# Row gathers and key projections moved across a branch in a single-core layer kernel

## The chip, the cores and the metric

The kernel runs on one core of a Trainium2 chip. A core has five engines with an instruction stream each: PE (TensorE, the matrix multiplier), DVE (VectorE), ACT (ScalarE), POOL (GpSimd) and SP (SyncE, which only issues transfers here). They meet through semaphores, and 16 DMA engines move data between the device memory (DRAM) and the core's on-chip memory. The metric is the device time of one execution in microseconds (us), as the median of several runs.

## The reference

The input is x, 4 sequences of 512 rows of 512 numbers (2048 rows), and a context of 4 x 512 rows of 256. Four blocks each add their result to x:

```python
x = x + ssm(ctx, layernorm(x))              # state space scan over the context
x = x + moe(layernorm(x))                   # 64 experts, 8 chosen for each row
x = x + attention(layernorm(x), ctx)        # 16 heads of 128, keys and values from ctx
x = x + ternary_ffn(layernorm(x))           # 512 -> 2048 -> 512, quantized weights
```

The change lies at the seam of the second and the third. In the second, each row has eight choices k = 0 to 7, and its result is a sum over them:

```python
y   = ragged_dot(silu(gate) * up, down)     # rows sorted by expert
out = zeros_like(x).at[tok].add(y * w[:, None])
```

In the third, keys and queries are projected, normalized by the root of their mean square over a head (gains gk and gq), and multiplied:

```python
q, k = rmsnorm(q, gq), rmsnorm(k, gk)
attn = softmax(einsum('bqhd,bkhd->bhqk', q, k) / sqrt(128))
out  = einsum('bhqk,bkhd->bqhd', attn, v) @ Wo
```

## The kernel before, in words

x stays on chip for the whole kernel as `x_all`, 16 tiles of 128 rows. The kernel goes through the state space block, then the routing, then a loop over experts (`Experts.run_in`, i = 0 to 65). In pass i it loads rows and weights of expert i + 2 by gathers on POOL (tiles `xg0`, `xg1`, `wg`, `wd`, four buffers each), multiplies gate and up for expert i - 1 (`gate_up`, L1343) and down for expert i - 2 (`down`, L1367 to L1389). The results are copied from the accumulators to tiles `yo` by DVE and ACT and stored by SP to a DRAM table `y_dram`, sorted by expert. An expert has room for a fixed number of rows.

Rows that did not fit are handled behind a branch: every engine loads the number `many` (L771) and takes the branch `tc.If(many > 0)` (L772) past that block, which is not executed with these inputs. On the way each engine waits for the transfers it depends on, and the first instructions behind the branch that share data wait until the other engines have passed it.

Then comes `attend`. It must first add the experts' results to x: for each tile t and choice k a gather on POOL brings 128 rows of `y_dram` (256 KB) into a tile `yg` (`fetch`, L1883), and DVE multiplies them by the router's weight and adds them to x (`add`, L1891). For the first four tiles these are 32 gathers and 32 additions. With all eight added, `stats` takes a tile's mean and variance on DVE (L1897, L1899) and the inverse deviation on POOL (`ve_c` L1901, `rstd_c` L1903), and `normed` writes `xn_c` on DVE (L1909).

A second kind of work fills PE meanwhile. The keys of sequences 2 and 3 for heads 8 to 15 (`KEYS_LATE`, 16 pairs) are left over from earlier. One key task is: the projection on PE (`pk`, L1223), its square `k_sq` and its scaled copy `k_kT` on ACT (L1232, L1233), a store of `k_kT` to `k_dram` (256 KB, L1234), the sums of squares on PE (`kpss`, L1243), and their copy `k_ms` on ACT (L1255). `k_sq` and `k_kT` are read out of the accumulator after pk, so kpss follows one task behind.

The order of the front of `attend` is written by hand: `later(time, f)` puts a step at a nominal time, the steps are sorted by it and issued in that order, so that each engine executes its part of them in that order, whatever the real times are. The plan has eight key tasks at a pace of 2.6 (`some_keys`), the gathers from 3.0 on at a pace of 1.35 (`GAP`), each addition 6.0 behind its gather (`FLIGHT`), and from 21.0 (`FRONT`) on four windows of 14.5 (`WINDOW`), one per tile of sequence 0. A window i holds `turn_x` (four transposes of xn_c, L1916), a key task, two projections of queries of four heads each (`queries`, L1962, with a 1 MB weight Wq for each), the norm of them (`norm_q`: `qms` on DVE, `rq` on POOL L1974; `scale_q`: `qn` on DVE L1980), their transposes (`turn_q`: `pqt` on PE L1989, copied to `qT` by ACT L1990), a second key task, and scores, softmax weights and their transposes for the first head (`scores` L1996, `weights`, `turn`). SP loads Wq for both groups (`load_q`), and keys, inverse norms and values of a head (`load_kv`: `kT`, `rk`, `v`, 256 KB each). Then the main loop over heads follows, and the ternary block is laid into it.

The first landing places of the gathers are four slices of a tile `yg_first` and eight of two tiles `yg_more`, which have other uses later; the others go through four buffers `yg`. `ms` holds the keys' mean squares of all sixteen late tasks.

Of the kernel before, what the change touches and what calls it, by code (L numbers as in the profile page):

```python
# [17 lines left out]
F32 = mybir.dt.float32  # L18
# [41 lines left out]
HG = 4  # L60

KEYS_LATE = [(b, h) for b in (2, 3) for h in range(8, H)]
DH = 2048
RESET = 1e30
MAGIC = 12582912.0
# [54 lines left out]
class Plan:  # L120
# [618 lines left out]
@with_exitstack  # L739
def moe_phase(ctx, cm, x_all, w, kv, dr, router_stats, out):  # L740

    tc, nc = cm.tc, cm.nc
    order = ctx.enter_context(ExitStack())
    order.enter_context(tc.manual_schedule())
    ssm_phase(cm, x_all, w, kv, router_stats)
    keep = ctx.enter_context(tc.tile_pool(name="b_keep", bufs=1))
    dp = ctx.enter_context(tc.tile_pool(name="b_dram", bufs=1, space=DRAM))
    y_dram = dp.tile([ROWS[E], DM], F32, name="y_dram")
    z_dram = dp.tile([NOV * P, DM], F32, name="z_dram")


    r = dict(wk=keep.tile([P, NT, TOPK], F32, name="wk"),
             pos=keep.tile([P, NT, TOPK], I32, name="pos"),
             nov=keep.tile([E, 1], F32, name="nov"),
             room=keep.tile([E, 1], F32, name="room"),
             many=keep.tile([1, 1], I32, name="many"))
    tern = Ternary(cm, keep, w)


    late = ctx.enter_context(tc.tile_pool(name="b_late", bufs=1))  # L760
    with ExitStack() as es:
        more = es.enter_context(tc.tile_pool(name="b_more", bufs=1))
        r["tok"] = more.tile([P, 3, E], I32, name="tok")
        r["widx"] = more.tile([P, E], I32, name="widx")
        keys = Keys(cm, w, kv, cm.k_small, None, None, None)
        with tc.tile_pool(name="e_w", bufs=4) as wp:
            ex = Experts(cm, w, dr, y_dram, r, wp)
            route(cm, x_all, w, dr, router_stats, r, more, late, keys, ex)
            ctx_k = ex.run(tern, more, late, keys, kv)
        order.close()  # L770
        many = nc.values_load(r["many"][0:1, 0:1], min_val=0, max_val=NOV)  # L771
        with tc.If(many > 0):  # L772
            rest(cm, x_all, w, dr["xn"], z_dram, r, many)
    with tc.manual_schedule():
        attend(cm, x_all, w, kv, y_dram, r["wk"], r["pos"], tern, late, ctx_k, keys.wk, out)


@with_exitstack
# [415 lines left out]
class Keys:  # L1194
# [6 lines left out]
    def __init__(self, cm, w, kv, small, row, psum, ctx, direct=None):  # L1201


        self.cm, self.nc, self.w, self.kv = cm, cm.nc, w, kv
        self.small, self.row, self.psum, self.ctx, self.direct = small, row, psum, ctx, direct
        self.wk = {}
        self.pk = self.sq = self.pss = None

    def load(self, h0, h1, pool, tag, queue=None):
# [17 lines left out]
    def evict(self):  # L1227
        if self.pk is None:
            return
        b, h, pk = self.pk  # L1230
        sq, kT = self.row("sq"), self.row("kT")
        self.nc.scalar.activation(sq, pk, AF.Square)  # L1232
        self.nc.scalar.activation(kT, pk, AF.Copy, scale=self.cm.gkq)  # L1233
        self.nc.sync.dma_start(self.kv["k"][b, h], kT)  # L1234
        self.pk, self.sq = None, (b * H + h, sq)

    def squares(self):
# [154 lines left out]
class Experts:  # L1392
# [20 lines left out]
        if FIRST <= i < E:  # L1413
            f(self.st[i])

    def run(self, tern, more, late, keys, kv):


        with ExitStack() as es:
            return self.run_in(es, tern, more, late, keys, kv)  # L1420

    def run_in(self, ctx, tern, more, late, keys, kv):
        cm, ex, st = self.cm, self.ex, self.st
        tc = cm.tc
        ex.sp = ctx.enter_context(tc.tile_pool(name="e_s", bufs=2))
        ex.yp = ctx.enter_context(tc.tile_pool(name="e_y", bufs=3))
        ex.ps = ctx.enter_context(tc.tile_pool(name="e_ps", bufs=2, space=PSUM))
        ex.pg = ctx.enter_context(tc.tile_pool(name="e_pg", bufs=3, space=PSUM))
        ex.po = ctx.enter_context(tc.tile_pool(name="e_po", bufs=3, space=PSUM))
        ex.tp = ctx.enter_context(tc.tile_pool(name="e_xt", bufs=1))  # L1430
        tp = ctx.enter_context(tc.tile_pool(name="e_t", bufs=2))
        ctx_k = late_contexts(keys, self.w, late)
        slots, norms = slot_tasks(cm, self.dr, kv, self.r, more, ex.ps)
        halves = tern.tasks(tp, ex.ps)
# [4 lines left out]
        held = []  # L1439
        QUOTA = 54  # L1440
        self.load_rows(0)
        self.load_rows(1)
        for i in range(E + 2):
            self.load_rows(i + 2)
            self.load_weights(i + 2)
            for m in range(3):
                if 1 <= i <= E:
                    ex.gate_up(st[i - 1], m)
                if m == 0 and held:
                    held.pop()()  # L1450
                if i < E and (i < FIRST or m < len(st[i]["n"]) - 1):
                    ex.turn_x(st[i], m)
            self.last(i, ex.join_last)
            self.last(i + 1, ex.turn_last)
            if i >= 2:
                ends = list(range(ROWS[i - 2], ROWS[i - 1], P)) + [ROWS[i - 1]]
                ex.down(st[i - 2], [self.y_dram[r0:r1, :] for r0, r1 in zip(ends, ends[1:])])
                while tasks and not held and done < (i - 1) * many / QUOTA:
                    left = tasks.pop(0)()
                    done += 1  # L1460
                    if left is not None:
                        held.append(left)
        assert not tasks and not held
        return ctx_k

# [383 lines left out]


@with_exitstack
def attend(ctx, cm, x_all, w, kv, y_dram, wk, pos, tern, late, ctx_k, wk_k, out):

# [19 lines left out]
    ks, vs, eTs, oTs, es = {}, {}, {}, {}, {}  # L1873


    rows = [(t, k) for t in range(NT) for k in range(TOPK)]
    ygs = []

    def fetch(n, into=None):
# [379 lines left out]


    n_ms = len(KEYS_LATE) * KB
    ms = pool[1].tile([P, n_ms], F32, name="k_ms")

    def key_row(n):

        if n == "sq":
# [3 lines left out]
    def key_bank(shape, name):  # L2270
        if name == "kpss":
# [1 line left out]
        return psc.tile(shape, F32, name=name, tag="psc")  # L2273

    keys = Keys(cm, w, kv, small, key_row, key_bank,
                lambda b: (ctx_k[b], 0), direct=ms)
    keys.wk = wk_k
    first = KEYS_LATE[0][1]

# [2 lines left out]
    def later(time, f, *a):  # L2282
        steps.append((time, len(steps), f, a))

    START, GAP, FLIGHT = 3.0, 1.35, 6.0
    FRONT, WINDOW = 21.0, 14.5

    wide = [pool[1].tile([P, KB, S], F32, name="yg_first", tag="eT")]
    wide += [pool[2].tile([P, HG, DM], F32, name="yg_more", tag="Wo") for _ in range(2)]
    places = [t[:, k] for t in wide for k in range(KB)]  # L2290
    for n in range(NC * TOPK):
        at = n % 16 - KB
        if n >= 16 and 0 <= at < KB:
            at = -1
        later(START + n * GAP, fetch, 1, places[at] if at >= 0 else None)
        later(START + n * GAP + FLIGHT, add, 1)

    left = list(KEYS_LATE)

    def key_task():  # L2300
        keys.task(*left.pop(0))
# [3 lines left out]
        keys.squares()  # L2305
        keys.take()

    def some_keys():
        keys.task(*left.pop(0))
        keys.squares()  # L2310
        keys.evict()
        keys.take()

    for i in range(H // 2):
        later(2.6 * i, some_keys)
    later(FRONT + 0.4, key_ends)
    for i in range(NC):
        end = START + ((i + 1) * TOPK - 1) * GAP + FLIGHT
        later(end + 0.1, stats, i, "c")
        later(end + 2.3, normed, i, "c")  # L2320
        at = FRONT + i * WINDOW
        later(at, turn_x, i)
        later(at + 0.5, key_task)
        later(at + 2.2, queries, 0, 0, i)
        later(at + 5.6, key_ends)
        later(at + 6.4, norm_q, 0, 0)
        later(at + 6.5, queries, 0, 1, i)
        later(at + 8.5, scale_q, 0, 0)
        later(at + 10, turn_q, 0, 0, i)
        later(at + 10.4, key_task)  # L2330
        later(at + 10.8, norm_q, 0, 1)
        later(at + 12.1, scores, 0, i)
        later(at + 12.9, scale_q, 0, 1)
        later(at + 13, key_ends)
        later(at + 14, turn_q, 0, 1, i)
        if i < KB - 1:
            later(at + 14.7, weights, 0, i)
        if i < KB - 2:
            later(at + 15, turn, 0, i)
    for f, n, time in ((load_q, 0, 9.5), (load_kv, 0, 14.5), (load_q, 1, 17.5), (load_kv, 1, 44),  # L2340
                       (load_kv, 2, 50)):
        later(time, f, n)
    for n in range(3):
        later(FRONT + (0, 2.5, 3.2)[n] * WINDOW + 9, norm_k, n, nc.vector)
# [208 lines left out]
```

## Time and profile before

| | us |
|---|---|
| median of three runs | 2471.33 |
| the three runs | 2467.07, 2478.49, 2471.33 |
| profiled execution, device time | 2469.94 |
| its span in the profile | 2468.2 |
| PE busy in the span | 2330.2 (94%) |
| last expert matmul on PE starts | 1292.09, takes 1.12 |
| first key task on PE starts (pk, L1223) | 1297.76 |
| first gather of `yg` issued | 1300.82 |
| first `turn_x` of a window on PE | 1329.61 |
| fourth window's end (main loop's first scores) | 1399.43 |

Times within the profile count from the span's start. A row of the timeline gives the start, the length, the engine and the line of an instruction or of a run of like ones, with the idle time of the engine before it and what ended that. A row of the waits says which instruction waited, for what, how long in all, how often and the longest. A row of the windows gives a stretch's busy time by engine, then the mean clock that PE was granted (1.00 is full speed), the share of time in which the DMA engines were busy and the rate in GB/s (1 GB/s is about 1 KB/us).

### The profile page before, as it was taken

To read this page: it belongs to the slowest core of one execution; us is meant where nothing else is said; L and a number is where in the kernel's file an instruction comes from. 1 tells how busy PE (TensorE), PEld (TensorE's weight loads), DVE (VectorE), ACT (ScalarE), POOL (GpSimd) and SP (SyncE) were. 2 spreads that over 40 slices of the span, in tenths; PEclk is the share of its full clock that TensorE was granted. 3 is DMA by queue.
4 is the path that set the end of the run, shared out by engine and by line. 5 is a ranking of instruction groups with operands and counts; after the bars stand their busy time and mean duration, and the time that the engine had idled before them with its cause. 6 is when DMAs were issued, how large, how long until landed. Compare 5 with 4: busy or idle time off the path is not lost. (4 is left out here: it accounts for less than half of the span.)

```text
span 2468.2 us, 29177 instructions
## 1 busy us (share of the span) xinstructions
PE 2330.2 (94%) x8819; PEld 1268.0 (51%) x8819; DVE 1590.2 (64%) x2872; ACT 1414.0 (57%) x2647; POOL 1332.1 (54%) x1314
## 2 busy tenths in 40 slices
PE   5989899988899999999998999999999999999998
PEld 2555555655555656666664444444444444444444
DVE  6999998956244434444324477667776778666655
ACT  6777777755333333344433466667666666667654
POOL 7999999940444434544426356356644655333323
PEclk8999998998999999999998999999999999999999
DMA  5362727343689868899976478678866887566530
GB/s 213 94 231 90 246 86 246 103 163 110 211 254 294 265 226 276 272 285 346 303 220 214 152 190 219 155 186 196 188 160 159 190 191 175 136 156 150 132 78 26
DMA packets 479892, 468.01 MB, mean 190 GB/s; under 512 B 313247, under 2 KB 354287, under 8 KB 475632
## 3 DMA queue, kind: packets, MB, share of 16 engines
q1 hardware_dynamic: 434686, 305.77, 46.3%
q0 software_dynamic: 42992, 160.13, 20.0%
q8 instruction: 72, 1.18, 0.2%
q14 instruction: 92, 0.75, 0.1%
q10 hardware_dynamic: 2050, 0.18, 0.1%
HBM read 316.11 MB, written 79.82 MB: 160 GB/s over the span
## 5 line engine op out<-in xcount | busy, mean ns | idle before, releaser
L1343 PE MATMUL pg<-xT,wg 128*128 128x284 f32 (+12 forms) x1536 | 389.4, 399 | 2.3 <-ACT xT L1310 1.3
L2027 POOL COPY planes<-e 128x512 int16<-128x512 int16 x174 | 119.2, 685 | 397.5 <-DVE e L2008 215.5
L1999 DVE TENSOR_REDUCE mx<-psc 128x1 f32<-128x512 f32 x256 | 176.3, 689 | 243.0 <-PE psc L1996 240.2
L1343 PEld LDWEIGHTS pg<-xT,wg 128*128 128x128 f32 x1536 | 280.4, 191 | 93.1 <-issue 40.2
L494 POOL TENSOR_TENSOR dBu<-bb,du 128x1024 f32<-128x1024 f32 x128 | 304.8, 2411 | 6.6 <-DVE dA L519 5.5
L2002 ACT ACTIVATE e<-psc,mx 128x512 f32<-128x512 f32 x256 | 176.3, 689 | 148.6 <-DVE mx L1999 77.6
L1996 PE MATMUL psc<-kT,qT 128*128 128x512 f32 x512 | 260.0, 594 | 0.0
L2068 PE MATMUL po<-eT,v 128*128 128x512 f32 x512 | 236.8, 605 | 13.5 <-ACT eT L2062 10.7
L1264 POOL DMA_INDIRECT xg<-xn_dram,tok x168 | 176.4, 1050 | 123.9 <-PE pt L1307 59.9
L1962 PE MATMUL pq<-Wq,xnT 128*128 128x512 f32 x512 | 231.8, 595 | 4.8 <-ACT xnT L1918 3.9
L2077 PE MATMUL px<-Wo,oT 128*128 128x512 f32 x512 | 231.2, 595 | 2.3 <-DVE qn L1980 2.3
L505 ACT ACTIVATE dA<-delta,negA 128x512 f32<-128x512 f32 x256 | 176.3, 694 | 50.9 <-DVE hc L520 37.3
L519 DVE TENSOR_TENSOR_SCAN dA<-dA,dBu 128x1024 f32<-128x1024 f32 x80 | 185.7, 2322 | 15.2 <-ACT dA L505 7.9
L1264 POOL DMA_INDIRECT wd<-down,widx x64 | 61.9, 967 | 225.1 <-PE po L1377 212.0
L2068 PEld LDWEIGHTS po<-eT,v 128*128 128x128 f32 x512 | 92.0, 189 | 150.7 <-issue 91.8
L1962 PEld LDWEIGHTS pq<-Wq,xnT 128*128 128x128 f32 x512 | 96.2, 190 | 129.8 <-issue 110.6
L2077 PEld LDWEIGHTS px<-Wo,oT 128*128 128x128 f32 x512 | 95.1, 190 | 125.5 <-issue 105.5
L525 PEld LDWEIGHTS yT<-ident,hc 128*128 128x128 f32 x1024 | 118.6, 143 | 74.5 <-issue 42.4
L1883 POOL DMA_INDIRECT yg<-y_dram,pos x108 | 118.1, 1094 | 59.0 <-issue 50.1
L1388 ACT COPY yo<-po 128x512 f32<-128x512 f32 (+3 forms) x64 | 37.5, 586 | 195.3 <-PE po L1377 150.5
L525 PE MATMUL yT<-ident,hc 128*128 128x128 f32 x1024 | 132.0, 276 | 17.6 <-DVE x_all L560 9.9
L1388 DVE COPY yo<-po 128x512 f32<-128x512 f32 x68 | 46.9, 691 | 151.3 <-PE po L1377 151.3
(380 smaller groups left out, 4696.6 us busy)
## 6 DMA issues: line engine op xcount, KB each, us to landing
y_dram<-yo SPq DMA_DIRECT2D x110, 256.0 KB
bb<-bc_dram SPq DMA_DIRECT2D x16, 1024.0 KB
cb<-bc_dram SPq DMA_DIRECT2D x16, 1024.0 KB
v_dram<-v SPq DMA_DIRECT2D x64, 256.0 KB
k_dram<-k_kT SPq DMA_DIRECT2D x64, 256.0 KB
kT<-k_dram SPq DMA_DIRECT2D x64, 256.0 KB
rk<-r_dram SPq DMA_DIRECT2D x64, 256.0 KB
v<-v_dram SPq DMA_DIRECT2D x64, 256.0 KB
```

Of the source, the lines that this page charges most:

```text
L494: nc.gpsimd.tensor_tensor(dBus[q], st[b]["bb"][i // 2][:, j:j + 2, :], st[b]["du"][c].unsqueeze(1).to_broadcast([P, 2, S]), ALU.mult)
L505: nc.scalar.activation(dAs[q][:, j, :], st[b]["delta"][c], AF.Exp, scale=negA[:, c, n:n + 1])
L519: nc.vector.tensor_tensor_scan(*flat, 0.0, ALU.mult, ALU.add)
L525: nc.tensor.matmul(yT[:, lc, :], t[:, lc * P:(lc + 1) * P], cm.ident, is_transpose=True, start=first and lc == 0, stop=last, skip_group_ch ...
L1264: nc.gpsimd.indirect_dma_start(out=t[0:n, :], out_offset=None, in_=table, in_offset=bass.IndirectOffsetOnAxis(ap=index, axis=0))
L1343: nc.tensor.matmul(pg[:, 0:n], s["wg"][:, c, m * P:(m + 1) * P], s["xT"][:, c, 0:n], start=c == 0, stop=c == NC - 1)
L1962: nc.tensor.matmul(pq.rearrange("p h d -> p (h d)"), xnTs[b * NC + i][:, c, :], s["Wq"][:, c, :], start=c == 0, stop=c == NC - 1)
L1996: nc.tensor.matmul(pscore, st[b, g]["qT"][:, h, i * P:(i + 1) * P], ks[n], start=True, stop=True)
L1999: nc.vector.tensor_reduce(mx, pscore, AX.X, ALU.max, negate=True)
L2002: nc.scalar.activation(e, pscore, AF.Exp, bias=mx, accum_out=tot)
L2068: nc.tensor.matmul(po, v[:, kc, :], eT[:, kc, :], start=kc == 0, stop=kc == KB - 1)
L2077: nc.tensor.matmul(px, oTs[j * HG + h][:, i * P:(i + 1) * P], st[b, g]["Wo"][:, h, :], start=h == 0, stop=h == HG - 1)
```

## The change

- 19 of the 32 gathers of the first four tiles are issued on POOL in the last passes of the expert loop, behind the last expert loads: four in pass 62, five in 63, six in 64, four in 65 (`EARLY`). Each reads the part of `y_dram` that can hold choice k (`ROWS[E - k]`). They land in the tiles `xg0` and `xg1`. Their additions are issued one pass later, ahead of the next gathers. All rows of tiles 0 and 1 and three of tile 2 are done so.
- Nine key tasks are issued in pass 65 in front of the branch (`first_keys`), in the experts' own accumulators and buffers; their stores are issued on ACT. The eight at the front of `attend` go. In the windows seven are left: the last window has one fewer.
- The other 13 gathers keep their pace of 1.35, from time 0 on; their additions stand 13 behind them instead of 6, and the gathers behind the first twelve, which use the buffers `yg`, later.
- `FRONT` is 3.5 instead of 21. Wq for both groups and the first keys and values are issued at 0, 3 and 3.5; the next keys and values at 30 and 36.
- The second `turn_q` of a window stands at 15.05 instead of 14, behind the next window's `turn_x` and first key task.

```diff
+FIRST_KEYS = 9
+EARLY = {E - 2: [(0, 7), (0, 6), (0, 5), (0, 4)],
+         E - 1: [(1, 7), (1, 6), (1, 5), (1, 4), (0, 3)],
+         E: [(1, 3), (0, 2), (1, 2), (2, 7), (2, 6), (2, 5)],
+         E + 1: [(0, 1), (0, 0), (1, 1), (1, 0)]}
...
-        self.nc.sync.dma_start(self.kv["k"][b, h], kT)
+        self.queue.dma_start(self.kv["k"][b, h], kT)
...
+    def early_rows(self, i):
+        r, ygs = self.r, []
+        for n, (t, k) in enumerate(EARLY.get(i, ())):
+            yg = gather(self.cm.nc, self.wp, f"xg{n % 2}", DM, self.y_dram[0:ROWS[E - k], :],
+                        r["pos"][:, t, k:k + 1])
+            ygs.append((yg, t, k))
+        return ygs
+
+    def add_rows(self, ygs, x_all):
+        for yg, t, k in ygs:
+            self.cm.nc.vector.scalar_tensor_tensor(
+                x_all[:, t, :], yg, self.r["wk"][:, t, k:k + 1], x_all[:, t, :], ALU.mult, ALU.add)
+
+    def first_keys(self, keys, kv, ctx_k, ms):
...
+        first = Keys(cm, self.w, kv, cm.k_small, row, bank, lambda b: (ctx_k[b], 0),
+                     direct=ms[:, 0:FIRST_KEYS * Keys.KB])
+        first.queue = cm.nc.scalar
+        first.wk = keys.wk
+        for b, h in KEYS_LATE[:FIRST_KEYS]:
+            first.task(b, h)
+            first.squares()
+            first.evict()
+            first.take()
+        first.squares()
+        first.take()
...
+            if i == E + 1:
+                self.add_rows(ygs, x_all)
+                ygs = self.early_rows(i)
+                self.first_keys(keys, kv, ctx_k, ms)
+            elif i > E - 3:
+                self.add_rows(ygs, x_all)
+                ygs = self.early_rows(i)
+        self.add_rows(ygs, x_all)
...
-    START, GAP, FLIGHT = 3.0, 1.35, 6.0
-    FRONT, WINDOW = 21.0, 14.5
+    GAP, FLIGHT = 1.35, 13.0
+    FRONT, WINDOW = 3.5, 14.5
...
-    for n in range(NC * TOPK):
-        at = n % 16 - KB
-        if n >= 16 and 0 <= at < KB:
-            at = -1
-        later(START + n * GAP, fetch, 1, places[at] if at >= 0 else None)
-        later(START + n * GAP + FLIGHT, add, 1)
+    ends = {}
+    for n, (t, k) in enumerate([tk for tk in rows if tk[0] < NC]):
+        at = n * GAP if n < len(places) + 4 else (n - 4) * GAP + FLIGHT + 0.05
+        later(at, fetch, 1, places[n] if n < len(places) else None)
+        ends[t] = at + FLIGHT
+        later(ends[t], add, 1)
...
-    for i in range(H // 2):
-        later(2.6 * i, some_keys)
-    later(FRONT + 0.4, key_ends)
...
-        later(end + 2.3, normed, i, "c")
+        later(max(end + 2.3, FRONT + (i - 1) * WINDOW + 0.1), normed, i, "c")
...
-        later(at + 10.4, key_task)
+        if i < NC - 1:
+            later(at + 10.4, key_task)
...
-        later(at + 14, turn_q, 0, 1, i)
+        later(at + 15.05, turn_q, 0, 1, i)
...
-    for f, n, time in ((load_q, 0, 9.5), (load_kv, 0, 14.5), (load_q, 1, 17.5), (load_kv, 1, 44),
-                       (load_kv, 2, 50)):
+    for f, n, time in ((load_q, 0, 0), (load_kv, 0, 3.5), (load_q, 1, 3), (load_kv, 1, 30),
+                       (load_kv, 2, 36)):
```

More of the change, by code (lines that the diff above doesn't have):

```diff
@@ L757, in moe_phase @@
     tern = Ternary(cm, keep, w)
+    ms = keep.tile([P, len(KEYS_LATE) * (S // P)], F32, name="k_ms")
     late = ctx.enter_context(tc.tile_pool(name="b_late", bufs=1))
@@ L768, in moe_phase @@
             route(cm, x_all, w, dr, router_stats, r, more, late, keys, ex)
-            ctx_k = ex.run(tern, more, late, keys, kv)
+            ctx_k = ex.run(tern, more, late, keys, kv, x_all, ms)
         order.close()
@@ L774, in moe_phase @@
     with tc.manual_schedule():
-        attend(cm, x_all, w, kv, y_dram, r["wk"], r["pos"], tern, late, ctx_k, keys.wk, out)
+        attend(cm, x_all, w, kv, y_dram, r["wk"], r["pos"], tern, late, ctx_k, keys.wk, ms, out)
 @with_exitstack
@@ L1206, in __init__ @@
         self.wk = {}
+        self.queue = self.nc.sync
         self.pk = self.sq = self.pss = None
@@ L1414, in last, with run, row, bank @@
             f(self.st[i])
-    def run(self, tern, more, late, keys, kv):
+    def run(self, tern, more, late, keys, kv, x_all, ms):
         with ExitStack() as es:
-            return self.run_in(es, tern, more, late, keys, kv)
-    def run_in(self, ctx, tern, more, late, keys, kv):
+            return self.run_in(es, tern, more, late, keys, kv, x_all, ms)
+    def early_rows(self, i):
[10 more added lines that the diff above has]
+    def first_keys(self, keys, kv, ctx_k, ms):
+        cm, ex = self.cm, self.ex
+        kTs = []
+        def row(n):
+            if n == "sq":
+                t = ex.sp.tile([P, 2, 3 * P], F32, name="k_sq", tag="sg")
+                return t.rearrange("p a s -> p (a s)")[:, 0:S]
+            if not kTs:
+                t = ex.sp.tile([P, NC, 3 * P], F32, name="k_kT", tag="xT").rearrange(
+                    "p c s -> p (c s)")
+                kTs.extend(t[:, j * S:(j + 1) * S] for j in range(3))
+            return kTs.pop(0)
+        def bank(shape, name):
+            return (ex.ps if name == "kpss" else ex.pg).tile(
+                shape, F32, name=name, tag="pt" if name == "kpss" else "pg")
+        first = Keys(cm, self.w, kv, cm.k_small, row, bank, lambda b: (ctx_k[b], 0),
[9 more added lines that the diff above has]
+        first.take()
+    def run_in(self, ctx, tern, more, late, keys, kv, x_all, ms):
         cm, ex, st = self.cm, self.ex, self.st
@@ L1438, in run_in @@
         done = 0
-        held = []
+        held, ygs = [], []
         QUOTA = 54
@@ L1851, in attend @@
 @with_exitstack
-def attend(ctx, cm, x_all, w, kv, y_dram, wk, pos, tern, late, ctx_k, wk_k, out):
+def attend(ctx, cm, x_all, w, kv, y_dram, wk, pos, tern, late, ctx_k, wk_k, ms, out):
     tc, nc = cm.tc, cm.nc
@@ L1873, in attend @@
     ks, vs, eTs, oTs, es = {}, {}, {}, {}, {}
-    rows = [(t, k) for t in range(NT) for k in range(TOPK)]
+    early = [tk for i in EARLY for tk in EARLY[i]]
+    rows = [(t, k) for t in range(NT) for k in range(TOPK) if (t, k) not in early]
     ygs = []
@@ L2261, in attend @@
     n_ms = len(KEYS_LATE) * KB
-    ms = pool[1].tile([P, n_ms], F32, name="k_ms")
     def key_row(n):
@@ L2275, in attend @@
     keys = Keys(cm, w, kv, small, key_row, key_bank,
-                lambda b: (ctx_k[b], 0), direct=ms)
+                lambda b: (ctx_k[b], 0), direct=ms[:, FIRST_KEYS * KB:])
     keys.wk = wk_k
@@ L2283, in later @@
         steps.append((time, len(steps), f, a))
-    START, GAP, FLIGHT = 3.0, 1.35, 6.0
-    FRONT, WINDOW = 21.0, 14.5
-    wide = [pool[1].tile([P, KB, S], F32, name="yg_first", tag="eT")]
-    wide += [pool[2].tile([P, HG, DM], F32, name="yg_more", tag="Wo") for _ in range(2)]
+    GAP, FLIGHT = 1.35, 13.0
+    FRONT, WINDOW = 3.5, 14.5
+    wide = [pool[2].tile([P, HG, DM], F32, name="yg_more", tag="Wo") for _ in range(2)]
     places = [t[:, k] for t in wide for k in range(KB)]
-    for n in range(NC * TOPK):
-        at = n % 16 - KB
-        if n >= 16 and 0 <= at < KB:
-            at = -1
-        later(START + n * GAP, fetch, 1, places[at] if at >= 0 else None)
-        later(START + n * GAP + FLIGHT, add, 1)
-    left = list(KEYS_LATE)
+    ends = {}
[4 more added lines that the diff above has]
+        later(ends[t], add, 1)
+    left = list(KEYS_LATE[FIRST_KEYS:])
     def key_task():
@@ L2306, in key_ends @@
         keys.take()
[L2308 to L2312, printed above, removed]
-    for i in range(H // 2):
-        later(2.6 * i, some_keys)
-    later(FRONT + 0.4, key_ends)
     for i in range(NC):
-        end = START + ((i + 1) * TOPK - 1) * GAP + FLIGHT
+        end = ends.get(i, 0)
         later(end + 0.1, stats, i, "c")
-        later(end + 2.3, normed, i, "c")
+        later(max(end + 2.3, FRONT + (i - 1) * WINDOW + 0.1), normed, i, "c")
         at = FRONT + i * WINDOW
```

## The prediction, made blind

> **What bounds the kernel now.** The page's busy list first, then the windows by stage, then what the tensor engine (PE) waited for in the stage that is edited, then that stage's rows in order of time.
>
> ```profile
> PE 2330.2 (94%) x8819; PEld 1268.0 (51%) x8819; DVE 1590.2 (64%) x2872; ACT 1414.0 (57%) x2647; POOL 1332.1 (54%) x1314
> ```
>
> PE is the bound, so an edit is worth what it takes out of PE's idle time, or out of PE's time at half clock. The edit touches the stretch between the end of PE's last expert matmul (1292.09 + 1.12 = 1293.21 us) and the end of the fourth query window (1399.43), 106.2 us. The rows of windows give us, then busy us and instructions of PE, PEld, DVE, ACT, POOL, then PE's granted clock, DMA share and GB/s:
>
> ```profile
> 1293.20:1399.40 106.20, 89.77 (x321) 50.33 (x321) 46.15 (x75) 37.62 (x79) 51.71 (x58) 0.90 0.53 167
> 1400.00:1500.00 100.00, 95.77 (x276) 43.79 (x274) 70.53 (x147) 61.40 (x130) 51.90 (x56) 1.00 0.78 211
> 1296.00:1300.00 4.00, 2.24 (x3) 1.18 (x4) 0.06 (x1) 0.00 (x0) 0.00 (x0) 0.57 0.22 59
> 1300.00:1304.00 4.00, 4.00 (x6) 1.54 (x5) 0.00 (x0) 1.28 (x2) 2.57 (x3) 0.58 0.30 74
> 1320.00:1324.00 4.00, 4.00 (x9) 1.93 (x9) 0.76 (x2) 0.49 (x2) 3.15 (x3) 0.52 0.99 360
> 1324.00:1328.00 4.00, 4.00 (x20) 2.57 (x20) 1.50 (x2) 2.08 (x6) 3.05 (x3) 1.00 0.86 290
> 1328.00:1332.00 4.00, 3.89 (x25) 2.91 (x24) 0.00 (x0) 1.98 (x5) 0.00 (x0) 1.00 0.85 224
> 1348.00:1352.00 4.00, 3.65 (x15) 2.95 (x16) 3.48 (x7) 1.76 (x3) 3.09 (x3) 0.60 0.53 158
> ```
>
> PE is idle for 106.20 - 89.77 = 16.4 us here, and its clock averages 0.90 against 1.00 in the hundred microseconds behind. The second loss comes behind the first: a clock near 0.5 follows the wait at the branch, the one at 1318 and the one at 1348. What PE waited for there:
>
> ```profile
> PE pqt L1989 <- DVE qn L1980: 5.3, 4, 2.8
> PE pk L1223 <- DVEq L772: 4.6, 1, 4.6
> PE kpss L1243 <- ACT k_ms L1255: 4.3, 1, 4.3
> PE kpss L1243 <- issue: 1.4, 1, 1.4
> PE pq L1962 <- DMA Wq<-Wq: 0.5, 1, 0.5
> ```
>
> and rows of the timeline (start, us, engine, line, and in brackets the idle time before):
>
> ```profile
> 1304.88 1.96 PE L1223 MATMUL pk<-k_ctx,k_w 128*128 128x512 f32 x4
> 1306.68 0.95 PE L1243 MATMUL kpss<-ones,k_sq 128*128 128x1 f32 x8
> 1307.49 1.96 PE L1223 MATMUL pk<-k_ctx,k_w 128*128 128x512 f32 x4
> ...
> 1329.61 0.63 PE L1916 MATMUL pt<-ident,xn_c 128*128 128x128 f32 x4
> ...
> 1384.46 0.60 PE L1916 MATMUL pt<-ident,xn_c 128*128 128x128 f32 x4
> ```
>
> The reader is to see a key task's undisturbed pace (1307.49 - 1304.88 = 2.61 us) and where a window starts (L1916): at 1329.61, 1349.25, 1366.90 and 1384.46. So the stretch is 4.55 us of branch, 31.85 us for eight key tasks (3.98 each, not 2.61), and windows of 19.64, 17.65, 17.56 and 14.97 us.
>
> **The change, part by part.**
>
> *Nine key tasks in front of the branch.* They follow the last expert matmul without the branch's 4.55 us. Nine pk start 2.61 apart: the last ends at 1293.3 + 8 x 2.61 + 1.96 = 1316.1, its k_sq on ACT (0.60) and last kpss (0.95) bring PE to about 1317.7. ACT has 0.60 + 0.69 + 0.17 = 1.46 us a task, and now issues the store too: its eight DMA issues at the kernel's start took 0.42 to 0.53, so some 1.95, under 2.61.
>
> *Nineteen gathers and adds ahead of them.* The vector engine's (DVE) adds, 19 x 0.75 = 14.3 us, lie in 1283 to 1305, where its rows are mostly idle. Five precede the last copy of expert results (1293.25), which moves by some 1.5 us, and so the last y_dram store (landed near 1300). The last four gathers wait for it: 4 x 1.25 + 2.5 to land + 4 adds, to about 1310. The GpSimd engine's (POOL) branch took 1267.78 to 1276.28, 8.5 us, and ends near 1315: all under the keys, costing nothing as long as it is passed by 1320. PE has no cover if an add holds h of expert 63: the four adds before h fit the 3.03 us of idle DVE before it, and its use at 1292.09 is 5 us later. Taken: 0; bounds -0.2 to 1.5.
>
> *What the branch costs now.* After it, SP's first Wq and POOL's first gather wait until all engines have passed, and SP passes once the last k_dram store has landed. Last k_kT: about 1316.1 + 0.60 + 0.69 + 0.1 = 1317.5. Store to landing: the last y_dram store, issued at 1296.7, had landed when POOL went on at 1299.7: 3.0. So 1320.5. Then POOL's one gather ahead of the statistics (0.8 until issue, 0.95), and from ve_c to the end of xn_c 1.97 (1316.59 to 1318.56): turn_x(0) at 1324.4 against 1329.61, **5.2 us gained**. Bounds: 7.1 (the store in 2 us, no wait before the gather) and 0 (the 33 us for which POOL waited show that a late store alone sets it).
>
> *Window 0.* The undisturbed length is window 3's, 14.97. PE's idle 1317.7 to 1324.4 is longer than any in front of the half clocks above, so half clock for one to two steps of 3.4 us: 1.7 to 3.4 lost, 2.2 taken. Wq(0), Wq(1) and kT, rk, v (2.75 MB) share the engines with eight gathers (2 MB). By the rates of 224 to 360 KB/us in the rows above, Wq(0) lands 6.3 to 9.3 us after issue (as its issue at 1317.71 did), at 1326.8 to 1329.8; needed 3.45 + some 2 of half clock behind turn_x, at 1329.8. Wq(1) comes with 4 MB at 1331.6 to 1338, needed near 1334.5; kT with 4.75 MB at 1333.7 to 1341.7, needed 14.1 behind turn_x, 1338.5. Waits 0 to 6; I take 2, since each middle lies at or a little behind its time of need. 15.0 + 2.2 + 2 = 19.2: **0.4 gained**, bounds +2.9 and -3.
>
> *turn_q moved behind turn_x, turn and the key task of the next window.* These give PE 0.63 + 0.6 + 1.96 = 3.2 us to do, more than the longest wait (2.78 in window 0, 1.5 in window 1). Behind it on ACT only its own copy (0.59) comes later, ahead of scores that are 9 us off. Five gathers are left in the windows, and the 13 later additions stand 13 us behind their gathers in the plan instead of 6: a late row (a landing takes 2.2 to 2.9) no longer holds up DVE's qms and qn, which queue behind it. Tile 3's last addition stands at 36.9 in the plan, its turn_x at 47: covered by 10 us; 0. I take 15.5 each (15.0 and 0.5 for the wait that windows 2 and 3 keep): **2.1 and 2.1 gained**; bounds 0 and 2.6 each.
>
> *One key task fewer in window 3:* 1.72 + 0.86 = **2.6 gained**; bound 0.6, if that task only covered a DVE wait.
>
> *Late instructions of ACT.* In 1308 to 1318 ACT idled 2.51, 2.69 and 3.12 us before k_ms and k_sq with their inputs ready, with DMA share 0.71 to 1.01: PE's 4.3 and 1.4. I charge one such spell, **-2.5**, bounds 0 and -8.
>
> **Sum:** 5.2 + 0.4 + 2.1 + 2.1 + 2.6 - 2.5 = 9.9 us off the profiled execution's 2469.94 (span 2468.2 and 1.7 around it): 2460.0. That execution is 1.4 below the median, 2471.33. PE is 96% busy behind the stretch, so what is gained there stays.
>
> A rule against the row: the Trainium skill ("TensorE: Matmul & The Clock Gate", "What's actually happening") says that half rate follows an idle window of about 3.4 us. The trace disagrees: 2.78 us before pqt at 1348.35 sufficed for 0.60 in 1348 to 1352. By the page a wait under 3.4 in a window costs only itself and the sum stays; by the row a 2.78 us wait that stays costs 1.4 more, 2461.4.
>
> **The rivals.**
>
> *Everything is in time* (full gain). Turn_x(0) at 1322.5, no Wq wait, one step of half clock, ACT never late: 7.1 + 2.9 + 2.6 + 2.6 + 2.6 = 17.8, 2452. For: DMA has fewer rows to bring. Against: the row of 0.99 share. About 2454 with one of these missing.
>
> *The wall behind the branch.* Loads, gathers, statistics start together at 1320.5, where before the keys covered them. Turn_x(0) at 1327, window 0 22.5, windows 1 and 2 17: 2.6 - 2.9 + 0.6 + 0.6 + 2.6 - 1 = 2.5, 2467.5. For: Wq(0) took 6 to 9 us beside gathers.
>
> *ACT sets the keys' pace* (slower). Nine tasks now run in one block with the store on ACT's own queue. At the eight tasks' former pace, 3.98, the keys end 9 x 1.37 = 12.3 later: 2460.0 + 12.3 = 2472.3; at the pace between the kpss of 1306.68 and of 1318.01 (two tasks, 5.67 each) 27.5 later, 2487.5. It decides from 2.61 + 9.9/9 = 3.7 us a task. For: those rows. Against: DMA carries 101 GB/s in 1290 to 1300, against 263 in 1310 to 1320, and the spells came with a full DMA. The Trainium skill ("Runtime: NRT & Kernel Launch", "Instruction fetch mechanics") has instructions fetched by DMA in sequence and a taken branch breaking that; PE's branch, 3.53 us, agrees, and the rule would put lateness behind the branch, not in the keys.
>
> *The gathers are not early after all:* if all 19 waited for the last store, POOL would issue until 1300 + 19 x 1.25 = 1324 and pass the branch at 1332: 2469. Against: the later choices (k = 7) need stores of experts long done.
>
> **How the numbers follow.** Forecast 0.42, full gain 0.25, wall (with late gathers) 0.19, ACT's pace 0.14. A measurement tells about 0.5%, 12.4 us, from no change: full gain and a third of the forecast's spread are beyond it (0.39); slower by it needs over 5 us a key task (0.11); 0.50 within. Range: 2452 (full gain) to 2473 (the former pace).
>
> **What would show it.** Right: pk follows po with under 1 us of idle time; turn_x(0) near 1324; one stretch of half clock behind it; pqt waits under 1 us; windows near 19, 15.5, 15.5, 12.4. Wrong: pk over 3 us apart with ACT idle before k_sq, PE waiting for Wq or for xn_c beyond 1327, a stall of PE within 1280 to 1293, or windows 1 to 3 at their old lengths.

## The result and the profile after

The changed kernel takes 2462.7 us in the median against 2471.33 before, 8.6 us less. The ratio over all runs is 0.997 with a 95% interval of 0.9958 to 0.9983, that is 7.4 us less (4.2 to 10.4): clear of zero, and under 0.5%. The forecast was 2460.0 in a range of 2452 to 2473, "within 0.5%" as the likeliest. The profiled execution took 2456.93 (span 2455.2).

The page's busy list of the changed kernel:

```profile
PE 2324.5 (95%) x8819; PEld 1264.5 (52%) x8819; DVE 1587.6 (65%) x2872; ACT 1413.3 (58%) x2647; POOL 1329.0 (54%) x1314
```

PE is busy for 5.7 us less with the same 8819 matmuls: less of its work ran at half clock (in the edited stretch it is busy for 84.34 us at a mean clock of 0.95, before for 89.77 at 0.90). Where the rest went is read from rows of PE's timeline (start, length, and in brackets the idle time before):

```profile
1290.31 1.12 PE L1384 MATMUL po<-wd,h 64*128 64x512 f32 x4
1291.36 3.70 PE L1230 MATMUL pk<-k_ctx,k_w 128*128 128x512 f32 x8
...
1313.17 1.90 PE L1250 MATMUL kpss<-ones,k_sq 128*128 128x1 f32 x16
1320.27 1.12 PE L1975 MATMUL pt<-ident,xn_c 128*128 128x128 f32 x4 [5.20 <-DVE xn_c L1968]
1321.18 3.62 PE L1230 MATMUL pk<-k_ctx,k_w 128*128 128x512 f32 x4
...
1336.70 0.64 PE L1975 MATMUL pt<-ident,xn_c 128*128 128x128 f32 x4
1339.35 1.08 PE L2120 MATMUL pet<-ident,e 128*128 128x128 f32 x4 [2.01 <-DVE e L2067]
1340.22 3.02 PE L1230 MATMUL pk<-k_ctx,k_w 128*128 128x512 f32 x4
...
1383.33 1.12 PE L2055 MATMUL psc<-kT,qT 128*128 128x512 f32 x2 [0.73 <-ACT qT L2049]
1386.13 0.63 PE L2048 MATMUL pqt<-ident,qn 128*128 128x128 f32 x4 [1.68 <-DVE qn L2039]
1386.59 1.02 PE L2055 MATMUL psc<-kT,qT 128*128 128x512 f32 x2
```

The stretch from the last expert matmul's end (1291.43) to the main loop's first scores (1386.59) is 95.16 us, where it was 106.22: 11.06 less. The whole span is 13.0 shorter (2468.2 against 2455.2); 1.78 of that lie ahead of the stretch (1293.21 against 1291.43) and 0.2 behind it. The first experiment shows that the code ahead varies by more than that from one execution to the next. The table has the stretch by stage in one profile of each kernel, with windows from one turn_x to the next:

| us | before | after | gained | predicted |
|---|---|---|---|---|
| last expert matmul to turn_x(0) | 36.40 | 28.84 | 7.56 | 5.2 |
| window 0 | 19.64 | 16.43 | 3.21 | 0.4 |
| window 1 | 17.65 | 18.94 | -1.29 | 2.1 |
| window 2 | 17.56 | 15.97 | 1.59 | 2.1 |
| window 3 | 14.97 | 14.98 | -0.01 | 2.6 |
| late instructions of ACT | | | 0 | -2.5 |
| sum | 106.22 | 95.16 | 11.06 | 9.9 |

The sum is close, and hardly a term is. The windows of time (busy us of PE, PEld, DVE, ACT, POOL, then granted clock, DMA share, GB/s), first of the whole stretch, show what follows the branch:

```profile
1291.40:1386.60 95.20, 84.34 (x323) 47.49 (x322) 40.82 (x69) 37.71 (x79) 36.76 (x46) 0.95 0.54 181
1316.00:1320.00 4.00, 0.00 (x0) 0.00 (x0) 0.33 (x1) 0.00 (x0) 2.05 (x5) 0.83 0.31 79
1320.00:1324.00 4.00, 3.73 (x8) 2.19 (x9) 0.84 (x2) 0.59 (x1) 3.22 (x4) 0.50 1.04 396
1324.00:1328.00 4.00, 4.00 (x8) 1.56 (x8) 0.00 (x0) 1.17 (x2) 3.09 (x4) 0.82 0.98 363
1336.00:1340.00 4.00, 1.99 (x15) 1.78 (x15) 3.93 (x8) 2.91 (x6) 2.11 (x3) 0.89 0.62 192
1340.00:1344.00 4.00, 4.00 (x13) 2.05 (x12) 3.15 (x6) 1.30 (x3) 1.20 (x2) 0.69 0.04 14
```

PE is idle for a whole row behind the keys and then runs at half clock, as forecast. The last two rows were not forecast: PE waits for DVE's softmax weights `e` in front of pet, with DVE busy for 3.93 of 4 us, and the clock drops again.

### The profile page after: what moved, and what is told of

Same layout as the page of the kernel before. It is cut to its first block, busy times and chain, and to the rows that moved or that the text cites. A ratio compares the mean times of both kernels' runs of the same rounds, so it can differ in the third digit from the quotient of the medians.

```text
span 2455.2 us, 29177 instructions
## 1 busy us (share of the span) xinstructions
PE 2324.5 (95%) x8819; PEld 1264.5 (52%) x8819; DVE 1587.6 (65%) x2872; ACT 1413.3 (58%) x2647; POOL 1329.0 (54%) x1314
## 5 line engine op out<-in xcount | busy, mean ns | idle before, releaser
L524 DVE TENSOR_TENSOR_SCAN dA<-dA,dBu 128x1024 f32<-128x1024 f32 x80 | 184.0, 2300 | 17.6 <-ACT dA L510 11.1
L2067 DVE TENSOR_SCALAR e<-e,tot 128x512 f32<-128x512 f32 x256 | 129.0, 504 | 13.5
```

What stands on the lines that cost most here:

```text
L524: nc.vector.tensor_tensor_scan(*flat, 0.0, ALU.mult, ALU.add)
```

## The experiments

Most readings below are of the stretch, stage by stage, in one profiled execution each, because the changed kernel's stretch repeats where the whole time does not. The first run shows that, and every profile that leaves the first stage as changed (the two of the changed kernel, r2, r8 and r10) has it at 28.84 to 28.86. The kernel before repeats less well (r5).

### The changed kernel a second time (r1)

No edit.

> The changed kernel, unaltered, as a second profiled execution, so that what repeats in the stretch from the last expert matmul to the end of the fourth window can be told from what one execution happened to show. The first one had 28.8 us until turn_x(0) and windows of 16.4, 18.9, 16.0 and 15.0, together 95.2 against 106.2 before. If the gain sits in the order of instructions, the stretch is again 95 +- 1.5 and the median 7 to 11 us below before. The rival, that the first execution was a lucky one (no late instructions of ACT): a stretch of 98 to 101 with ACT idle before k_sq or k_ms with its input ready, somewhere behind the branch.

Measured: 28.85 to turn_x(0), windows of 16.45, 18.96, 15.97 and 14.99, a stretch of 95.21. Every stage is within 0.02 us of the first execution. Ratio to the kernel before 0.9951 (0.993 to 0.9972). So the new waits come with this order of instructions and are no chance of one execution. The end of the last expert matmul lay at 1297.52 this time, 6.1 later than in the first execution: the code ahead of the stretch varies by more than most of the terms studied here.

### The kernel before a second time (r5)

No edit.

> The kernel before, unaltered, as a second profiled execution. The stretch from the last expert matmul to the end of the fourth window took 106.2 in the first, with ACT idle before k_ms and k_sq three times (2.5 to 3.1 us) while its inputs were ready. If these spells belong to the order of the work, the stretch is again 106 +- 1; if they are chance, it is 100 to 104 with the key tasks nearer to 2.61 us each, and the gain of the change is by so much smaller.

Measured: 27.65 to turn_x(0), not 36.40, and windows of 27.38, 18.27, 15.87 and 14.97: a stretch of 104.13. ACT was late nowhere; the keys ran at 2.61 from the third one on. What PE waited for between 1291 and 1400, before in its second execution:

```profile
PE pq L1962 <- DMA Wq<-Wq: 7.1, 1, 7.1
PE pk L1223 <- DVEq L772: 4.6, 1, 4.6
PE pqt L1989 <- DVE qn L1980: 3.5, 3, 1.5
```

and its windows of time around that wait, and then, from the timeline, the issue of the second Wq and its first use:

```profile
1328.00:1332.00 4.00, 3.90 (x24) 2.78 (x23) 1.71 (x4) 1.98 (x5) 3.08 (x4) 1.00 1.02 364
1332.00:1336.00 4.00, 4.00 (x11) 1.83 (x10) 2.48 (x4) 1.18 (x2) 3.09 (x4) 1.00 1.04 387
1336.00:1340.00 4.00, 1.69 (x11) 1.12 (x9) 2.77 (x5) 0.77 (x2) 1.72 (x3) 1.00 1.05 402
1340.00:1344.00 4.00, 0.00 (x0) 0.00 (x0) 3.13 (x6) 0.00 (x0) 3.49 (x5) 0.54 0.93 345
```

```profile
1328.55 1.36 SPq L1926 DMA_DIRECT2D Wq<-Wq  x1
1344.83 1.22 PE L1962 MATMUL pq<-Wq,xnT 128*128 128x512 f32 x1 [7.14 <-DMA Wq<-Wq]
```

The second Wq was on its way for 16 us beside the gathers, under a DMA share of 1.0. Both executions are 104 to 106 long, once by late keys and once by a late Wq. The late ACT of the first profile was therefore no property of the order, and with it neither was the pace of 3.98 us a key.

The table above is to be read with this. Against the second profile of before, the changed kernel gains -1.19 up to turn_x(0), then 10.95, -0.67, -0.10 and -0.01 in the windows, 9.0 in all. The sum is much the same, and it lies in another stage: the first stage gains only against a profile in which ACT was late.

### The order of the Wq loads alone (r9)

```diff
 # kernel before
-((load_q, 0, 9.5), (load_kv, 0, 14.5), (load_q, 1, 17.5), ...
+((load_q, 0, 0), (load_kv, 0, 14.5), (load_q, 1, 3), ...
```

> The kernel before with one edit, the order of the two Wq loads: at 0 and 3 in the plan, ahead of the gathers, as in the changed kernel, instead of 9.5 and 17.5. In its second profiled execution the kernel before had keys at 2.61 with ACT never late, turn_x(0) already 27.7 us behind the last expert matmul, and then waited 7.1 us for the second Wq, issued at 1328.6 and landed at 1344.8 under a DMA share of 1.0. Theory: what bounds the stretch before is the transfers (32 gathers, two Wq, keys and values in one place), and the late second Wq is where it shows; with both Wq first the wait for it goes, and a stretch of 97 to 100 follows. Rival: the same bytes in the same time only delay the rows, and turn_x of windows 0 to 2 waits in its place: 103 to 106.

Measured, in one profile: 27.75, then 20.98, 19.37, 16.86, 14.97: a stretch of 99.92, at the upper edge of the theory's 97 to 100. In its waits Wq no longer appears:

```profile
PE pqt L1989 <- DVE qn L1980: 5.7, 5, 3.1
PE pk L1223 <- DVEq L772: 4.6, 1, 4.6
PE pt L1916 <- DVE xn_c L1909: 0.6, 1, 0.6
```

Two numbers in the plan take 4.2 to 6.3 us out of the stretch, about half of what the whole change gains there. In the whole time this does not show: 0.9987 (0.9961 to 1.0014). Some of the wait did move, to qn (3.1) and to the rows (0.6).

### The early gathers alone (r6)

```diff
 # changed kernel
-FIRST_KEYS = 9
+FIRST_KEYS = 0
-                self.first_keys(keys, kv, ctx_k, ms)
-    FRONT, WINDOW = 3.5, 14.5
+    FRONT, WINDOW = 21.0, 14.5
+    for i in range(H // 2):
+        later(2.6 * i, some_keys)
+    later(FRONT + 0.4, key_ends)
```

The fourth window has its second key task again, and load_kv(1) and (2) stand at 44 and 50.

> The 19 early gathers and additions alone: no key task in front of the branch, eight behind it at the plan's old pace, then windows as in the kernel before with turn_q as changed. Theory: DVE and POOL reach the branch only behind their 19 additions and gathers, some 19 to 20 us behind PE's last expert matmul (in the changed kernel DVE passed at 1313.0, PE had ended the experts at 1291.4), and the first pk behind the branch waits for them; then eight key tasks at 2.61 and 1.7 to 3.4 lost to half clock: turn_x(0) 43 to 46 us behind the last expert matmul (before 36.4, changed 28.8), windows of 15 to 16.5, 18.9, 16, 15: a stretch of 109 to 112, 3 to 6 us over before. Rival, that the early rows are the gain and the keys' place is not: the keys run at 2.61 from 4.6 on, turn_x(0) at 27 to 30, a stretch of 94 to 97.

Measured: pk 18.93 behind the last expert matmul, turn_x(0) at 41.04, windows of 15.13, 16.87, 16.26 and 15.44: 104.75, and a ratio of 1.0024 (1.0003 to 1.0045).

```profile
PE pk L1230 <- DVE half L1926: 18.9, 1, 18.9
```

The mechanism is as expected: `half` is DVE's first instruction behind the branch, and DVE reaches it only after its additions. The price was some 4 us lower than expected, since the keys then ran without disturbance and the windows were short. Alone, this half of the change is worth nothing. This kernel also has both Wq loads first, as r9 has, and against r9's 99.92 its stretch is 4.8 longer.

### The keys in front of the branch alone (r7)

```diff
 # changed kernel
-EARLY = {E - 2: [(0, 7), ...], ...}
+EARLY = {}
-    GAP, FLIGHT = 1.35, 13.0
-    FRONT, WINDOW = 3.5, 14.5
+    GAP, FLIGHT = 1.35, 6.0
+    FRONT, WINDOW = 18.1, 14.5
```

load_kv(1) and (2) stand at 44 and 50.

> The nine key tasks in front of the branch alone: all 32 gathers behind it, additions 6 behind their gathers in the plan, windows from 18.1 on. Theory: the rows of tile 0 are then in nobody's shadow. The first gather leaves some 26 us behind the last expert matmul, twelve gathers at 1.25 to 1.3 stand ahead of tile 0's statistics on POOL, so turn_x(0) at 26 + 15.5 + 2.5 = 44 (before 36.4, changed 28.8), PE idle for 19 us, and windows of 17 to 19 with the rest of the rows in them, 14.98 for the fourth: a stretch of 111 to 115, 5 to 9 over before. Rival, that the keys' place makes the gain (branch and late ACT): turn_x(0) below 36 and a stretch below 104.

Measured: 46.25 to turn_x(0), windows of 16.24, 22.27, 21.05 and 14.99, a stretch of 120.80, more than expected; ratio 1.0117 (1.0069 to 1.0165).

```profile
PE pt L1972 <- DVE xn_c L1965: 23.0, 2, 22.6
PE pet L2117 <- DVE e L2064: 7.5, 2, 4.3
```

PE waits 22.6 us for the first tile's rows. Alone this half costs some 15 us of the stretch (21 against r9, which shares its early Wq loads). The two halves only pay together: the gathers need PE's keys to hide under, and the keys leave nothing behind the branch for late rows to hide under.

### turn_q back in its place (r8)

```diff
 # changed kernel
-        later(at + 15.05, turn_q, 0, 1, i)
+        later(at + 14, turn_q, 0, 1, i)
```

> The changed kernel with the second turn_q of a window back at 14, in front of the next turn_x. Theory: moving it gained nothing, since the wait moved to pet behind it (2.0 and 1.0): with it back PE waits at pqt for qn (1 to 2.8) and pet finds e ready; the stretch is 95 +- 1. Rival, my prediction's term: each of windows 1 and 2 is 2.1 longer, a stretch of 99.

Measured: 28.84, windows of 18.34, 17.92, 15.86 and 14.51: 95.47. In this order of the rest, the move is worth 0.3 us. Its wait is back at pqt, and the 2.0 at pet is gone:

```profile
PE pqt L2048 <- DVE qn L2039: 2.4, 4, 1.2
PE psc L2055 <- ACT qT L2049: 0.7, 1, 0.7
PE pet L2120 <- ACT qT L2049: 0.5, 2, 0.2
```

### turn behind the next key task (r2)

```diff
 # changed kernel
-            later(at + 15, turn, 0, i)
+            later(at + 15.02, turn, 0, i)
```

> The changed kernel with the transposes of the softmax weights (turn, pet) moved from 15 to 15.02 in the plan, behind the next window's first key task. Theory: in windows 1 and 2 PE waits for DVE's e in front of pet (2.0 and 1.0 us) because moving turn_q away left turn there with only turn_x to cover the softmax chain; the key task's 1.8 us covers it, and the half clock behind the first of the waits (about 1.2 us) goes too. Windows 1 and 2: 18.9 to some 15.6, 16.0 to some 15.0; 4 us less than the changed kernel. Rival: DVE is behind as a whole there (busy 3.93 of 4 us), so the wait goes to the pqt or pq behind: 0 to 1 us less.

Measured: 28.85, windows of 16.62, 16.35, 14.75 and 14.98: 91.54, so 3.6 less than the changed kernel. Ratio to the kernel before 0.9927 (0.9901 to 0.9954). The waits at pet shrink to 0.3:

```profile
PE pqt L2048 <- DVE qn L2039: 2.6, 2, 1.7
PE psc L2055 <- ACT qT L2049: 0.7, 1, 0.7
PE pet L2120 <- DVE e L2067: 0.3, 1, 0.3
```

DVE was not the limit; pet only stood one key task too early.

### Eight key tasks in front (r3)

```diff
 # changed kernel
-FIRST_KEYS = 9
+FIRST_KEYS = 8
-        if i < NC - 1:
-            later(at + 10.4, key_task)
+        later(at + 10.4, key_task)
```

> The changed kernel with eight key tasks in front of the branch instead of nine, and the fourth window's second one back. Theory: in the fourth window the missing task had covered waits, and PE now waits 0.7 for qT and 1.7 for qn in its place; so the block in front is 2.6 us shorter, the fourth window stays at 15.0, and the stretch is 2.6 us shorter (92.6). Rival, my prediction's accounting, that PE's work counts wherever it stands: the fourth window of the changed kernel is short of one task, with it back it is 17 to 17.6 long, and the sum is unchanged, 95.

Measured: 26.32, windows of 16.11, 18.78, 15.97 and 15.44: 92.63, the theory's number. With the task back, window 3 is 0.46 longer and the block in front 2.52 shorter. Ratio 0.9954 (0.9934 to 0.9973), which cannot be told from the unaltered kernel's.

### Both (r4)

The edits of r2 and r3 together.

> Both edits together, turn behind the key task and eight key tasks in front. If each takes out a wait of its own: 4 + 2.6 = 6.6 us less than the changed kernel, a stretch of 88.6 and a median some 14 to 16 us below before. If DVE is the limit in the windows, the fewer tasks in front only bring DVE's waits forward: 2.6 or less.

Measured: 26.80, windows of 15.60, 16.40, 14.75 and 15.44: 88.98 where 88.6 was expected. The two waits add up. Ratio 0.9949 (0.9921 to 0.9976).

### The additions 6 instead of 13 behind their gathers (r10)

```diff
 # changed kernel
-    GAP, FLIGHT = 1.35, 13.0
+    GAP, FLIGHT = 1.35, 6.0
```

> The changed kernel with the 13 later additions 6 instead of 13 behind their gathers in the plan. Theory, my prediction's: moving them back was worth nothing either way, the rows land 2.2 to 2.9 us after their issue; the stretch is 95 +- 1, with the second window a little shorter since the additions leave it. Rival: rows under a DMA share of 1.0 land late, DVE waits for them ahead of qms and qn, and the first window is 2 to 4 longer: 97 to 99.

Measured: 28.86, windows of 18.39, 22.54, 16.27 and 14.98: 101.04, 5.9 more than the changed kernel. The theory falls. The rival was right for the first window, 2.0 longer; but the second is 3.6 longer besides. DVE's and PE's rows of this kernel:

```profile
1322.90 0.75 DVE L1950 SCALAR_TENSOR_TENSOR x_all<-yg_more,wk,x_all 128x512 f32<-128x512 f32 x1 [2.22 <-DMA yg_more<-y_dram,pos]
1325.78 0.75 DVE L1950 SCALAR_TENSOR_TENSOR x_all<-yg_more,wk,x_all 128x512 f32<-128x512 f32 x1 [2.12 <-DMA yg_more<-y_dram,pos]
1328.77 0.75 DVE L1950 SCALAR_TENSOR_TENSOR x_all<-yg_more,wk,x_all 128x512 f32<-128x512 f32 x1 [2.24 <-DMA yg_more<-y_dram,pos]
...
1340.11 0.69 DVE L2039 TENSOR_TENSOR qn<-pq,rq 128x512 f32<-128x512 f32 x1 [2.90 <-POOL rq L2033]
...
1342.69 0.49 DVE L2067 TENSOR_SCALAR e<-e,tot 128x512 f32<-128x512 f32 x1
1343.32 1.08 PE L2120 MATMUL pet<-ident,e 128*128 128x128 f32 x4 [5.46 <-DVE e L2067]
```

and POOL's around rq:

```profile
1333.76 0.79 POOL L1960 TENSOR_SCALAR ve_c<-mv_c 128x1 f32<-128x1 f32 x1
1334.63 1.05 POOL L1962 TENSOR_TENSOR rstd_c<-ve_c,half 128x1 f32<-128x1 f32 x1
1335.87 1.58 POOL L1942 DMA_INDIRECT yg<-y_dram,pos  x1 [0.19 <-issue]
1337.75 0.96 POOL L1942 DMA_INDIRECT yg<-y_dram,pos  x1 [0.30 <-issue]
1338.73 0.22 POOL L2032 TENSOR_SCALAR qms<-qms 128x4 f32<-128x4 f32 x1
1339.03 1.05 POOL L2033 TENSOR_TENSOR rq<-qms,half 128x4 f32<-128x4 f32 x1
```

`FLIGHT` sets the place of the statistics too (and of the last of the 13 gathers), so they also stand 7 earlier in the plan. DVE takes up the first rows as they land, one every 3 us, and the third holds up qms: it starts 10.6 us behind turn_x(0), in the changed kernel 9.0. That is the first window. Tile 2's statistics also come in window 0, where the changed kernel has them in window 1. On POOL these (ve_c, rstd_c) now stand in front of rq, with two gathers: rq starts 20.2 us behind turn_x(0), in the changed kernel 15.8. DVE sits in front of qn for 2.9 us, and e is queued behind qn, so pet comes 24.5 us behind turn_x(0) instead of 19.1.

### Statistics ahead of the first gather (r11)

```diff
 # both, and
-        at = n * GAP if n < ...
+        at = 0.15 + n * GAP if n < ...
```

> The changed kernel with turn behind the next key task and eight key tasks in front (88.98 as measured with these two), and the first gather behind the branch put behind the statistics of tiles 0 and 1 on POOL. Expected: rstd no longer waits for the gather's 0.94, so turn_x(0) comes 1 us earlier, 25.8, and the stretch is 88 if later rows are still in time; 89 or more if they are not.

Measured: turn_x(0) at 23.38, 3.4 earlier than with both (expected 1), but window 0 is 19.74, 4.1 longer: 89.29. What was gained is waited for at the first Wq:

```profile
PE pt L1975 <- DVE xn_c L1968: 2.4, 1, 2.4
PE pq L2021 <- DMA Wq<-Wq: 2.0, 1, 2.0
```

Ratio 0.9961 (0.9943 to 0.998). Why turn_x(0) came 3.4 and not 1 us earlier can be read from the rows of POOL and SP, first with both edits only (r4), then here:

```profile
1322.43 0.94 POOL L1942 DMA_INDIRECT yg_more<-y_dram,pos  x1 [11.35 <-SPq L778]
1323.45 0.24 POOL L1960 TENSOR_SCALAR ve_c<-mv_c 128x1 f32<-128x1 f32 x1
```

```profile
1318.88 0.24 POOL L1960 TENSOR_SCALAR ve_c<-mv_c 128x1 f32<-128x1 f32 x1 [9.20 <-DVE mv_c L1958]
1321.52 0.96 SPq L1985 DMA_DIRECT2D Wq<-Wq  x2
```

In r4 the gather in front of ve_c waits for SP to pass the branch, and SP waits for the last store. The statistics need only DVE's mv_c, and here they run 2.6 us ahead of SP's first load. The edit took the wait for SP out of their way, and not only the gather's own 0.94.

### A key task ahead of turn_x(0) (r12)

```diff
 # the one before, and
-        later(at + 0.5, key_task)
+        later(at + 0.5 if i else at - 0.1, key_task)
-        later(at + 5.6, key_ends)
+        later(at + 5.6 if i else at + 0.1, key_ends)
```

load_kv(0) stands at 3.2 instead of 3.5.

> The one before, and the first key task behind the branch moved ahead of turn_x(0), with the first keys and values loaded before its store. PE waits 5.3 to 5.8 for xn_c there; pk needs only that all engines have passed the branch, some 2 us behind the last kpss. Expected: of the 5.3 us about 3 are filled and half clock lasts no longer, turn_x(0) unmoved at 26, the first window 2 to 3 shorter, a stretch of 85 to 86. Rival: the first Wq lands only as late as the queries need it now, and the wait moves to pq: 88.

Measured: 24.21, windows of 18.70, 15.97, 14.74 and 15.44: 89.06. The rival's 88 is nearest: the gap in front of turn_x(0) is filled, and the queries wait for Wq instead.

```profile
PE pq L2021 <- DMA Wq<-Wq: 2.7, 2, 2.4
PE pk L1230 <- ACTq L778: 1.4, 1, 1.4
```

Ratio 0.9942 (0.992 to 0.9965). Three versions with both edits thus have a stretch of 89, against 95.2 and 104 to 106. Their ratios to the kernel before lie apart from 1, but their intervals overlap those of the changed kernel, so that they beat it is shown for the stretch, not for the whole time.

## Why the prediction was right or wrong

The forecast time and direction held. The stretch gained 11.1 against the first profile of before and 9.0 against the second, and 9.9 was the sum. That it came so near is partly luck: against the first profile the terms are off by 2.4, 2.8, -3.4, -0.5, -2.6 and 2.5, and these cancel down to 1.2.

**Nine key tasks in front: right.** pk starts 0.07 us before the last expert matmul's modelled end, the pace is 2.61, PE is done 23.6 us behind the experts (24.5 predicted). ACT, with the store on its own queue (0.33 an issue), still idled 0.86 us before each k_sq, so the rival of ACT's pace had nothing to stand on.

**Gathers and additions hidden: right.** The four additions in front of h (the product silu(gate) * up, which down multiplies) ended as h began, the last yo copy moved by 1.3 us, POOL reached the end of its branch at 1309.9 and then waited for SP until 1316.7. Nothing of it reached PE.

**From the branch to turn_x(0): the chain right, the gain not.** 5.2 was forecast. The first profiles give 7.56, beyond even the favourable bound of 7.1; the second profile of before, without late ACT, gives -1.19. The chain ran as described, and r11 shows that the gather's wait for SP is what holds it. Its terms were too long: the last k_dram store left 23.1 us behind the experts instead of 24.3 (the first two pk follow each other without a kpss between them); issued at 1314.57, it had released SP at 1316.62 (2.05 us, 3.0 taken); and from ve_c to the end of xn_c it took 1.49, not 1.97. Only the time from the release to the gather was longer, 1.1 instead of 0.8. (The terms as written add up to 1324.2, not 1324.4.)

**Window 0: half right.** Half clock cost what was said (pt, pk and the first pq together 2.7 us over their full-speed lengths, 2.2 taken), but no wait for Wq came (2 taken): PE used the first Wq 7.1 us behind its issue and did not wait. In r11 and r12, where turn_x(0) comes 3.4 and 2.6 us earlier than in r4, PE does wait, and Wq is there 5.5 and 5.1 us behind its issue, where the prediction had 6.3 to 9.3. The base was also too long: with turn_q moved out, the window has 0.6 less to do. What the prediction did not price is the place of the Wq loads in the kernel before: r9 shows that their order alone is worth 4.2 to 6.3 us of the stretch.

**turn_q moved: wrong.** The step reads "These give PE 0.63 + 0.6 + 1.96 = 3.2 us to do". One of the three, turn, was itself waiting: for e, whose chain of scores, maximum, exponential and division takes 4.4 us (psc at 1334.94, pet at 1339.35), with only kpss and turn_x between them. turn_q's own wait had hidden that. The move gained 0.3 (r8) instead of 4.2 for the two windows; putting pet behind the key task gained 3.6 (r2).

**The additions moved back: named, not priced.** The prediction said that a late row would no longer hold up qms and qn, put the cost of the move at 0 and no gain on it. It is worth 5.9 (r10). The mechanism it named is window 0's part, 2.0. More comes by a way that it had not seen, 3.6 in window 1: the statistics, which move with the additions, stood on POOL in front of rq, and qn and e wait behind it. The landing time was also too short: behind the branch the rows for `yg_more`, where the trace shows their landing, took 6.6 to 7.2 us from the start of their issue, where an issue of 0.95 and a landing of 2.2 to 2.9 had been taken. Without this unpriced gain the stretch would have fallen short of the sum.

**One key task fewer in window 3: wrong.** 2.6 was taken, and the window did not get shorter (14.97 and 14.98). Since the moved turn_q of window 2 has come into it, r3 is the cleaner comparison: with the task back, the window is 0.46 longer. That is the case of the bound of 0.6, a task that only covered a DVE wait: the waits of 0.73 for qT and 1.68 for qn in the rows above stand in its place. In front of the branch the same task costs 2.5.

**Late instructions of ACT: wrong, as a price.** The spells of the first profile did not come back in the second one of before nor in the changed kernel. The prediction took the 31.85 us for eight keys, which hold these spells, as the length to be gained on, and charged one spell, 2.5, to the changed kernel. The second execution shows the other limit, 8 MB of rows and 2 MB of Wq in one place. How often ACT is late is open.

**The rivals.** The wall behind the branch did not come: that rival had turn_x(0) 33.8 us behind the experts and a window 0 of 22.5, and 28.84 and 16.43 were measured. Of the full gain the first two terms came in full (7.56 and 3.21 for 7.1 and 2.9, against the first profile); it failed in windows 1 to 3, on waits that the edit itself made. ACT's pace did not rule the keys, which kept 2.61. That the gathers are not early is refuted: POOL took the branch at 1303.7 with all 19 issued.

**The clock.** The Trainium skill's page "TensorE: Matmul & The Clock Gate" ("What's actually happening") asks for an idle window of some 3.4 us before half rate. Behind 2.01 us of waiting at pet the clock fell to 0.69 in 1340 to 1344; pet took 1.08 instead of 0.63 and pk 3.02 instead of 1.88. As in the profile of before, the trace disagrees: the wait cost 1.6 us on top of itself, near the 1.4 that the prediction had by the row.

## What to carry to other kernels

A wait that is moved off one instruction goes to the next one in that engine's order that depends on the same slow chain: before pricing a move, follow every instruction that is brought forward back to its own producer. Work of the busiest engine may be cover for another engine's chain; taking it out of a window that waits anyway gains little (0.46 us here), and where nothing waits it costs its full length (2.5 us). One profile can show a stall that the next does not have, so before a stall is built into a sum, look for a second limit (here a transfer at full DMA share) that would hold the stretch just as long without it.

## What the runs showed of the hardware

- The edited stretch repeated to 0.05 us in the changed kernel (106.22 and 104.13 in the kernel before), while the end of the experts lay between 1289.98 and 1309.34 and the part behind the stretch took 1063 to 1073 over the fourteen profiles (both kernels and these twelve), nearly all of it in code that no edit touched. A gain of a few microseconds is read from the stretch; the medians of whole executions hide it.
- PE's own branch instruction took 3.45 to 3.53 us in every profile in which it follows the last expert matmul directly (before twice, r9, r6), and 0.35 in all ten in which key tasks stand between. The Trainium skill's page "Runtime: NRT & Kernel Launch" ("Instruction fetch mechanics") says that a taken branch costs a fetch when its target is not among the pages held. That would allow for both, but no run here shows which pages were held.
- In the changed kernel two 1 MB loads of Wq issued together behind the branch cost PE nothing with eight gathers beside them (PE used the first 7.1 us behind its issue). In the kernel before, the second Wq, issued in the midst of the gathers, was used 9.9 us behind its issue in one profile (1328.03 to 1337.97, after a wait of 0.5 us) and 16 us in the other, after a wait of 7.1.
